# A decoder layer with an order written out by hand: another period string, idle products at both ends, and a first norm on two engines

## The chip, the core and the metric

The kernel runs on one core of a Trainium2 chip. A core has a matrix engine (TensorE, here PE, with its weight loads shown apart as PEld), a vector engine (VectorE, DVE), an activation engine (ScalarE, ACT), a general engine (GpSimd, POOL) and a queue processor that here only issues DMAs (SyncE, SP). Each engine works through its own instructions strictly in the order of the program, and waits for another engine by semaphores. The metric is the device time of one execution in microseconds (us); lower is better. Before the change the median of three runs is 2741.01 us (2739.99 to 2745.0).

## The reference

The input x is 128 sequences of 128 tokens with 256 features, all in float32. The layer does three things, each added to x: self-attention, cross-attention to a context of the same size, and a feed-forward part with 1024 hidden features. Each begins with a layer norm without weights.

```python
x = x + attn(layernorm(x), Wq, bq, Wk, bk, Wv, bv, Wo, bo)         # 16 heads of 16 features
x = x + xattn(layernorm(x), ctx, ctx, mask, wq, ..., wo_b)         # masked scores become 1e-9
x = x + ffn(layernorm(x), W_fc, ln_w, ln_b, W_proj)

# attention, per head: softmax(q k^T / 4) v, all heads side by side, then the output product
# ffn: weights are made ternary (-1, 0, 1) by their mean absolute value
h = gelu(x @ ternary(W_fc).T)
h = layernorm(h, ln_w, ln_b)
return h @ ternary(W_proj).T
```

## The kernel before

**Tiling.** Four sequences make a group; there are 32 groups. A group's x lies in SBUF as 128 tokens by 4 sequences by 256 features. Within a group, attention is done sequence by sequence (a "row"), for all 16 heads at once: the heads' score products use only 32 rows of the array each, so that four of them run side by side in four strips of the array (lines 680, 691, 752, 776); the product with the values (line 797) uses 32 columns each. All other products use the whole array.

**Streams.** The work is written as Python generators, "streams". Each `yield` ends a step, and each stream has one letter:

- `A`: attention, all rows of all groups in turn. A row's steps are `maxima` (scores, and their row maxima by DVE, line 702), `outputs` of the row before (line 797, copied out by ACT, line 800), `transposed_scores` (line 752) with `weights` (ACT's exponential, line 785), and `transposed_maxima` (line 719). Self rows of a group and cross rows of the group before it alternate by fours.
- `n`: `prepare_self`: load x, norm and transpose it (`transposed_copy`), then queries, keys and values. 17 steps a group.
- `k`: `prepare_keys`: load the context, then keys and values. 9 steps a group.
- `c`: `prepare_cross`: finish self-attention (`projected`: divide by the sums, output product, add to x), norm, and make the cross queries. 14 steps a group.
- `f`: `finish`: finish cross-attention, norm, then `hidden` (product and gelu) and `second` (norm of the hidden features, transposes, product), store. 36 steps a group. It runs for all groups but the last.
- `x`, `y`, `z`: the same for the last group, in three pieces of its rows (`finish_rows`).
- `w`, `t`: constants, and the ternary weights, once.

**Order.** Every engine's program is the order in which the steps are taken. This order is a string of letters: `START`, then `ORDER` once for each group of the middle, then `END` (line 851). `ORDER` has 112 letters, one group's worth of every stream: 36 A, 36 f, 17 n, 14 c, 9 k. Nothing else decides what comes before what. If an operand is late at a step, PE stands still, since the next step's products stand behind it in its queue.

**What joins the streams besides data.** All whole-array products and transposes take their output bank from one pool of three PSUM banks (`bank`, line 187). The fourth claim has to wait until the first bank is emptied by ACT or DVE. Scores have two tiles of their own, and the value product and the transposed maxima share one bank (`ps_av`). DVE empties the score tiles (line 702), copies values (line 365), adds products to x (lines 411, 503), makes the low halves of split operands (lines 425, 481), and computes the norms' statistics (lines 268, 269). POOL turns variances into reciprocal deviations (lines 274, 275) and applies the norms (line 279, four instructions for the four sequences of a group). SP issues all DMAs.

**The beginning.** The first group's x is loaded first. `transposed` takes its statistics in two steps, has POOL compute the deviations and apply the norm to the four sequences in the third, and then transposes the result on PE (line 297) in two steps.

Of the kernel before, what the change touches and what calls it, by code (L numbers as in the profile page):

```python
# [27 lines left out]
P = 128  # L28
# [21 lines left out]

START = (
    "nnnnnnwnwnnnwnnnAnAAnnAwnAAnAnAnAAAAAnnAAknnwAnnnnwnccnkAnnAAnnAnAkAcccckcAAcAnAAkccAccccntAAkAAnkAn"
    "AnAAnAkckAnnAnAcAnAnAnntAnAAAckccAccckkAAknAkAnknAnckcnAcAActAAftkAAAncAcAAntAAAffffAffnAnfnAnnAAnAn"
    "kAffnAAkfcfAffkfAAfknncffAAffffAkkfAnfcAcnfAfAffAAccfAc"
)
ORDER = (
    "ncfAfffAAkkAccAAcfcAnnfAAAccAffAAnnkAAnnAnfAnkAAAfffAfffnAAkcnnAnnAnAfkfkcAffffffAAfffAfffAfccccfffA"
    "fkfkAAAncfAn"  # L60
)
END = (
    "cfAfAffAfAcAcffcAfAAckAAxcAkcfffAAfffAAkfAAAAAkffkAcfAcAfffffAffAffccfffAcckcfckfAffAfAkkAfcAcfAAffc"
    "cAcfcAfAfkAAffAkAkfkAAAAfAfAffffAAxxAffAxAfffAxfffyfAfffffyfxAyffffAfxyxxxzxyfxfffzffyxzzffxxxxyyzxx"
    "yyzzzyzzz"
)


# [1 line left out]
def tile_decoder_layer(ctx: ExitStack, tc: tile.TileContext, a: dict, out: bass.AP):  # L70
    nc = tc.nc
    n_groups = a["x"].shape[0] // G
# [16 lines left out]
    def load_group(b):  # L89
        x = p_in.tile([P, G, D], F32, name="x", tag="x")  # L90
        nc.sync.dma_start(x, a["x"][b * G : (b + 1) * G].rearrange("g s d -> s g d"))
        held[b] = x
# [52 lines left out]
    ident = const.tile([P, P], F32, name="ident")  # L145
# [41 lines left out]
    def bank(name):  # L187
        return ps_mm.tile([P, 512], F32, name=name, tag="mm")
# [44 lines left out]

    def constants():

        attention_biases(w_self, "attn")
        yield
        output_bias(w_self)
        yield
        attention_biases(w_cross, "xattn")  # L240
        yield
        output_bias(w_cross)
        yield
        masks()
        yield

        row_of = const.tile([P, 4], F32, name="row_of")
        for n in range(4):  # L250
            rows = ident_strips[:, :, n:12:4]
            nc.vector.tensor_reduce(row_of[:, n : n + 1], rows, AX.XY, ALU.add)
            nc.vector.tensor_copy(add_max[:, n], row_of[:, n : n + 1].to_broadcast([P, P]))
        for i in range(2):
            rows = ident_strips[:, :, 4 * (i + 1) : 12]
            nc.vector.tensor_reduce(minus[:, i : i + 1], rows, AX.XY, ALU.add, negate=True)
        nc.gpsimd.memset(negms["cross"], 0.0)
        for v in values[1:]:
            clear_values(v)
        yield  # L260


    def statistics(src, rows, n, agg, at=0):
        for i, j in enumerate(rows):
            pieces = max(1, n // 512)
            stats = p_stat.tile([P, pieces, 6], F32, name="stats", tag="stats")
            for k in range(pieces):
                nc.vector.bn_stats(stats[:, k], src[:, j, k * n // pieces : (k + 1) * n // pieces])  # L268
            nc.vector.bn_aggr(agg[:, at + i], stats.rearrange("p i s -> p (i s)"))  # L269

    def deviation(agg, g):

        rstd = p_stat.tile([P, g], F32, name="rstd", tag="rstd", bufs=6)
        nc.gpsimd.tensor_scalar(rstd, agg[:, :, 1], LN_EPS, None, ALU.add)  # L274
        nc.gpsimd.tensor_tensor(rstd, rstd, minus_half.to_broadcast([P, g]), ALU.pow)
        return rstd

    def apply(engine, dst, src, agg, rstd, j):
        engine.tensor_scalar(  # L279
            dst[:, j], src[:, j], agg[:, j, 0:1], rstd[:, j : j + 1], ALU.subtract, ALU.mult  # L280
        )

    def transposed(x, evacuate):

        agg = p_stat.tile([P, G, 2], F32, name="agg", tag="agg", bufs=6)
        statistics(x, (0, 1), D, agg)
        yield
        statistics(x, (2, 3), D, agg, 2)
        rstd = deviation(agg, G)
        xn = p_act.tile([P, G, D], F32, name="xn", tag="xn", bufs=1)  # L290
        for j in range(G):
            apply(nc.gpsimd, xn, x, agg, rstd, j)
        yield
        for c in range(CC):
            pt = bank("pt")
            for j in range(G):
                nc.tensor.transpose(pt[:, j * P : (j + 1) * P], xn[:, j, c * P : (c + 1) * P], ident)  # L297
            evacuate(c, pt)
            if c == 0:
                yield  # L300

    def transposed_copy(x):
        xn_t = []

        def evacuate(c, pt):
            if c == 0:
                xn_t.append(p_act.tile([P, CC, T], F32, name="xn_t", tag="xn_t"))
            nc.scalar.copy(xn_t[0][:, c], pt)

        yield from transposed(x, evacuate)  # L310
        return xn_t[0]

    def product_halves(w, o, src_t, name):
# [55 lines left out]
    def queries(w, xn_t, unit):  # L369
        for o in range(CC):  # L370
            pq = yield from product_halves(w["q"], o, xn_t, "pq")
            if o == 0:
                qt = unit["q"] = p_act.tile([P, CC, T], F32, name="qt", tag="qt", bufs=3)
            nc.scalar.activation(qt[:, o], pq, AF.Identity, bias=w["bq"][:, o : o + 1], scale=Q_SCALE)
            if o == 0:
                yield
# [169 lines left out]
    def prepare_self(b):  # L546
        if b:
            load_group(b)
        yield
        x = held[b]  # L550
        xn_t = yield from transposed_copy(x)
        yield
        unit = ready["self", b] = {}
        yield from queries(w_self, xn_t, unit)
        yield
        yield from keys_values(w_self, xn_t, unit)
        add_row(x, w_self["bo"])
# [255 lines left out]
    def attention():  # L813
        w_t = added = None
        for i in range(-1, 2 * G * (n_groups + 1) + 1):
# [17 lines left out]
            if cross and here:  # L833
                w_t = weights(here[0], s, added_here)
                yield

    def all_groups(steps_of_group, groups=n_groups):
        for b in range(groups):
            yield from steps_of_group(b)
            yield  # L840
# [4 lines left out]
        "k": all_groups(prepare_keys),  # L845
        "c": all_groups(prepare_cross),
        "f": all_groups(finish, n_groups - 1),
        "w": constants(),
        "t": ternary_weights(),
    } | {letter: finish_rows(j0, n_rows) for letter, j0, n_rows in PIECES}  # L850
    for letter in START + ORDER * (n_groups - 4) + END:
        next(streams[letter])

    assert all(next(stream, None) is None for stream in streams.values())
# [42 lines left out]
```

## Time and profile before

| view | value |
|---|---|
| median of the runs | 2741.01 us |
| profiled execution, device time | 2739.6 us |
| its span, first to last instruction | 2737.6 us |
| PE busy | 2676.8 us (98%) |
| DVE busy | 2115.0 us (77%) |
| ACT busy | 1577.8 us (58%) |
| POOL busy | 1337.7 us (49%) |
| mean granted PE clock | 0.998 |

The profiled execution took 2739.6 us, 2.0 us more than its span and 1.4 us less than the median of the runs. A busy share is an average over the beginning, the 28 middle periods and the end. Matmuls are pipelined, and their ends are modelled: a PE that is shown as busy may still be held up for a few tenths of a microsecond. So PE's work is better read from one step's start to the next one's start.

The page cuts the span into 40 slices of 68 us: PE is busy nine tenths or more in all but the first (seven) and the last two (eight). DMAs keep the 16 DMA engines busy for a fifth of the time.

### The profile page before, as it was taken

The page shows a single profiled execution, that of the slowest core. Times are in us where ns is not written, and L with a number is a line of the kernel's source. Part 1 is how long each engine was busy: PE and PEld are TensorE (multiplying, and loading weights), DVE is VectorE, ACT ScalarE, POOL GpSimd, SP SyncE. Part 2 cuts the span into 40 slices and gives each one's busy share as a digit, 9 for nine tenths or more (in the row PEclk, how much of TensorE's full clock was granted, in tenths as well). Part 3 has the DMA queues.
Part 4 walks back from the last instruction along what each step waited for, and adds up shares of the span by engine and source line. Part 5 has one row for each costly group of instructions (what it writes and reads, how often), then busy time and mean ns, then how long its engine had stood idle before and what let it go on. Part 6 is the DMA issues. An engine that isn't in the chain of part 4 may idle for free.

```text
span 2737.6 us, 77047 instructions
## 1 busy us (share of the span) xinstructions
PE 2676.8 (98%) x32845; PEld 1917.6 (70%) x32845; DVE 2115.0 (77%) x3914; ACT 1577.8 (58%) x2508; POOL 1337.7 (49%) x1427
## 2 busy tenths in 40 slices
PE   7999999999999999999999999999999999999988
PEld 4567777777777777776777776777776777777666
DVE  4677787777887777887777887777877778877777
ACT  3455665655665556666556666556666556656546
POOL 2344554544554444554445545445545445545443
PEclk9999999999999999999999999999999999999999
DMA  4121111221121221122211212211112211212210
GB/s 110 41 50 35 46 44 49 57 56 31 46 48 50 57 49 35 41 53 53 57 42 41 42 49 57 57 42 41 42 49 58 57 32 47 47 49 50 50 26 16
DMA packets 110045, 130.28 MB, mean 48 GB/s; under 512 B 32264, under 2 KB 69000, under 8 KB 109704
## 3 DMA queue, kind: packets, MB, share of 16 engines
q1 hardware_dynamic: 109704, 125.37, 19.0%
q8 instruction: 259, 4.24, 0.6%
q14 instruction: 82, 0.67, 0.1%
HBM read 71.38 MB, written 18.84 MB: 33 GB/s over the span
## 4 chain that ended last, share of the span: by engine, by line
PE 89%; DVE 7%; issue 2%; POOL 1%; ACT 1%; DMA 0%; DVEq 0%; ACTq 0%; POOLq 0%; SPq 0%
PE st L752 10%; PE av L797 9%; PE pq L317 9%; PE s L691 9%; PE ph L436 9%; PE py L494 8%; PE pk L317 8%; PE po L329 8%; PE pv L329 8%; PE pt L297 3%; PE pg L470 2%; PE s L680 2%; PE st L776 2%; DVE mx L702 1%; DVE g L481 1%
## 5 line engine op out<-in xcount | busy, mean ns | idle before, releaser
L702 DVE TENSOR_REDUCE mx<-s 128x8 f32<-128x1024 f32 x512 | 601.0, 1215 | 82.2 <-PE s L691 81.8
L785 ACT ACTIVATE w_t<-st 128x1024 f32<-128x1024 f32 x512 | 496.7, 1022 | 200.7 <-PE st L776 121.4
L274 POOL TENSOR_SCALAR rstd<-agg 128x4 f32<-128x4 f32 (+2 forms) x163 | 38.8, 238 | 969.0 <-DVE agg L269 964.7
L279 POOL TENSOR_SCALAR xn<-x,agg,rstd 128x256 f32<-128x256 f32 x380 | 459.4, 1222 | 9.9
L762 DVE COPY_PREDICATED_SCALAR st<-masked_t,masked_score 128x1024 f32 x256 | 316.1, 1280 | 67.7 <-PE st L752 67.6
L407 POOL TENSOR_TENSOR o_raw<-o_raw,factors 128x256 f32<-128x256 f32 x252 | 181.3, 745 | 382.3 <-DMA factors<-by_head 277.7
L800 ACT COPY raw<-av 128x512 f32<-128x512 f32 x256 | 150.7, 589 | 314.7 <-PE av L797 306.9
L479 ACT ACTIVATE g<-pg,ln_w 128x256 fp32r<-128x256 f32 (+1 forms) x520 | 205.4, 472 | 175.6 <-PE pg L470 163.3
L691 PE MATMUL s<-kt,qt 32*128 32x256 f32 x4096 | 298.0, 401 | 3.2 <-ACT w_t L785 2.2
L494 PE MATMUL py<-w_proj,g 128*128 128x256 f32 x2048 | 279.6, 289 | 1.3 <-DVE g L481 0.8
L797 PE MATMUL av<-w_t,v 128*32 128x128 f32 x8192 | 277.8, 276 | 0.5 <-DVE q_max L724 0.5
L797 PEld LDWEIGHTS av<-w_t,v 128*32 128x32 f32 x8192 | 209.6, 110 | 97.3 <-issue 80.5
L436 PE MATMUL ph<-w_fc,xn 128*128 128x512 f32 x1024 | 259.6, 403 | 5.2 <-ACT g L443 2.6
L494 PEld LDWEIGHTS py<-w_proj,g 128*128 128x128 f32 x2048 | 254.0, 189 | 13.2 <-issue 1.3
L279 POOL TENSOR_SCALAR g<-g,agg,rstd 128x1024 f32<-128x1024 f32 x63 | 241.1, 3826 | 6.6
L481 DVE SCALAR_TENSOR_TENSOR g<-pg,ln_w,g 128x256 fp32r<-128x256 f32 (+1 forms) x520 | 212.5, 469 | 30.5 <-ACT g L479 30.3
L691 PEld LDWEIGHTS s<-kt,qt 32*128 32x128 f32 x4096 | 187.0, 184 | 63.2 <-issue 39.7
L436 PEld LDWEIGHTS ph<-w_fc,xn 128*128 128x128 f32 x1024 | 184.5, 188 | 59.9 <-DVE xn L425 10.3
L752 PEld LDWEIGHTS st<-q_max,kt 32*128 32x128 f32 x4096 | 129.2, 186 | 61.0 <-DVE negm_self L713 42.5
L268 DVE BATCH_NORM_STATS2 stats<-g 128x6 f32<-128x512 f32 x256 | 160.9, 670 | 0.8 <-ACT g L443 0.8
L443 ACT ACTIVATE g<-ph 128x512 f32<-128x512 f32 x256 | 146.5, 599 | 25.8 <-PE ph L436 24.5
L752 PEld LDWEIGHTS st<-qt,kt 32*128 32x128 f32 x4096 | 128.1, 186 | 46.3 <-DVE mx L702 26.4
(129 smaller groups left out, 4610.6 us busy)
## 6 DMA issues: line engine op xcount, KB each, us to landing
o_raw<-raw SPq DMA_DIRECT2D x504, 64.0 KB
factors<-by_head SPq DMA_DIRECT2D x126, 256.0 KB
x<-in_x_dram SPq DMA_DIRECT2D x32, 512.0 KB
ctx_t<-in_ctx_t_dram SPq DMA_DIRECT2D x32, 512.0 KB
out_dram<-x SPq DMA_DIRECT2D x31, 512.0 KB
sums<-raw SPq DMA_DIRECT2D x126, 16.0 KB
by_head<-r SPq DMA_DIRECT2D x63, 32.0 KB
raw_w<-in_w_fc_t_dram SPq DMA_DIRECT2D x1, 1024.0 KB
```

Of the source, the lines that this page charges most:

```text
L279: engine.tensor_scalar(dst[:, j], src[:, j], agg[:, j, 0:1], rstd[:, j : j + 1], ALU.subtract, ALU.mult)
L317: nc.tensor.matmul(out, w[:, c, o * P : (o + 1) * P], src_t[:, c], start=(c == 0), stop=(c == CC - 1))
L329: nc.tensor.matmul(rows[:, j], src_t[:, c, (j0 + j) * P : (j0 + j + 1) * P], w[:, c], start=(c == 0), stop=(c == CC - 1),)
L436: nc.tensor.matmul(ph, xn_parts[i][:, c, (j0 + j - at) * P : (j0 + j - at + 1) * P], w_fc[:, c, n * 512 : (n + 1) * 512], start=((i, c) == ...
L481: nc.vector.scalar_tensor_tensor(parts[1][:, f0 + f, tok], pieces[:, f], scales[f], parts[0][:, f0 + f, tok].bitcast(F32), ALU.mult, ALU.s ...
L494: nc.tensor.matmul(rows[:, j], parts[i][:, f, j * P : (j + 1) * P], w_proj[:, f], start=((i, f) == terms[0]), stop=((i, f) == terms[-1]),)
L691: nc.tensor.matmul(s[r // 2][:, r % 2, 2 * o : 2 * o + 2], qt[strip, o, tok], kt[strip, o, :, tok], start=(stage == "self"), stop=True, sk ...
L702: nc.vector.tensor_reduce(mx[:, 2 * half : 2 * half + 2], s[half], AX.X, ALU.max, negate=True)
L752: nc.tensor.matmul(s[r // 2][:, r % 2, n], kt[strip, n // 2, n % 2, tok], added[strip, n // 2, n % 2] if stage == "self" else qt[strip, n ...
L762: nc.vector.copy_predicated(s[half].rearrange("p r n q -> p (r n) q"), masked_t[:, None, :].to_broadcast([P, 8, P]), masked_score[:, :, No ...
L785: nc.scalar.activation(w_t[:, 2 * half : 2 * half + 2], s[half], AF.Exp)
L797: nc.tensor.matmul(av[32 * r : 32 * r + 32, n], v[:, j, head : head + 32], w_t[:, r, n], start=True, stop=True)
```

## The change

There are three parts.

1. **The strings.** `START`, `ORDER` and `END` are all replaced. The new `ORDER` again has 36 A, 36 f, 17 n, 14 c and 9 k, in another sequence, and the streams stand in other phases to each other when it begins: the new `START` takes 89 A, 70 n, 35 c, 23 k and 21 f (before: 89 A, 68 n, 35 c, 23 k, 29 f). `ORDER` is run 27 times rather than 28, and `END` has 335 letters rather than 209, since one more group is in it.
2. **Idle products.** A new stream `d` appears 30 times in `START` and 8 times in `END`, never in `ORDER`. A step of it takes a bank from the pool of three and does four transposes of the identity matrix into it. Nothing reads the result.
3. **The first group's norm.** For group 0 in `prepare_self` the norm is applied by DVE and POOL in turn (sequences 0 and 2 by DVE, 1 and 3 by POOL). All other groups keep POOL alone.

```diff
 START = (
-    "nnnnnnwnwnnnwnnnAnAAnnAwnAAnAnAnAAAAAnnAAknnwAnnnnwnccnkAnnAAnnAnAkAcccckcAAcAnAAkccAccccntAAkAAnkAn"
...
+    "ndddnddnnnwdnnnnnnnnwknwAnddAAdnndnAdndndAAddAAwnndAAndAAnAAAdwdnAnnnwnntncnAddnkcAAkndAtkknAAccccAc"
...
 ORDER = (
-    "ncfAfffAAkkAccAAcfcAnnfAAAccAffAAnnkAAnnAnfAnkAAAfffAfffnAAkcnnAnnAnAfkfkcAffffffAAfffAfffAfccccfffA"
-    "fkfkAAAncfAn"
+    "kcfAAkkAfAkffcAcfffAAcncfAAfffAAccAffAAfknAfnfAAnnAAnfnAcnAnnnAffAAfAfncAfnfkkAAccAcAcnAncffAAfnffff"
+    "fAffffnAkAkf"
 )
 END = (
...
-    "yyzzzyzzz"
+    "fAfcdAAAffdfAffAkkAffAfAccfffAccAcfAncffAAAAnAdAAfffnAffAfnfnkcnnckAAnffnAfffAffccfkAccfnAAfcnAffAfA"
...
+    "AcfcfckkcfkkfAfAffcfAkkcffccccfAAfAAffAfAAAAAAfffAfdffAAdxxdAffAxAdffxfAfffAffffffyydAfyxffffAfyxxxz"
+    "xfxxfyffzffyzzyxffzxxxxzzxyxyyzyzzz"
 )
...
-    def transposed(x, evacuate):
+    def transposed(x, evacuate, engines=(nc.gpsimd,)):
...
-            apply(nc.gpsimd, xn, x, agg, rstd, j)
+            apply(engines[j % len(engines)], xn, x, agg, rstd, j)
...
-        xn_t = yield from transposed_copy(x)
+        engines = () if b else ((nc.vector, nc.gpsimd),)
+        xn_t = yield from transposed_copy(x, *engines)
...
+    def idle_products():
+        for _ in range((START + END).count("d")):
+            rows = bank("idle")
+            for j in range(4):
+                nc.tensor.transpose(rows[:, j * P : (j + 1) * P], ident, ident)
+            yield
...
+        "d": idle_products(),
...
-    for letter in START + ORDER * (n_groups - 4) + END:
+    for letter in START + ORDER * (n_groups - 5) + END:
```

More of the change, by code (lines that the diff above doesn't have):

```diff
@@ L53 @@
 START = (
-    "nnnnnnwnwnnnwnnnAnAAnnAwnAAnAnAnAAAAAnnAAknnwAnnnnwnccnkAnnAAnnAnAkAcccckcAAcAnAAkccAccccntAAkAAnkAn"
-    "AnAAnAkckAnnAnAcAnAnAnntAnAAAckccAccckkAAknAkAnknAnckcnAcAActAAftkAAAncAcAAntAAAffffAffnAnfnAnnAAnAn"
-    "kAffnAAkfcfAffkfAAfknncffAAffffAkkfAnfcAcnfAfAffAAccfAc"
+    "ndddnddnnnwdnnnnnnnnwknwAnddAAdnndnAdndndAAddAAwnndAAndAAnAAAdwdnAnnnwnntncnAddnkcAAkndAtkknAAccccAc"
+    "cAnkkAAAkkdccAccncctAAkkAAtdnAnAnAAnnAAcnnAncAAnAAnkAdcAAAcccAknccAkAAknAnAnnkAnccndAAAkkAAccfAnAcnA"
+    "cnAAntAfAAffAfkfAfAnfdnAAdAnkAcdnkAAffnAnnAnAfffAcffkAAnAncfAkcAAcfcAfdAfAnnffc"
 )
 ORDER = (
-    "ncfAfffAAkkAccAAcfcAnnfAAAccAffAAnnkAAnnAnfAnkAAAfffAfffnAAkcnnAnnAnAfkfkcAffffffAAfffAfffAfccccfffA"
-    "fkfkAAAncfAn"
+    "kcfAAkkAfAkffcAcfffAAcncfAAfffAAccAffAAfknAfnfAAnnAAnfnAcnAnnnAffAAfAfncAfnfkkAAccAcAcnAncffAAfnffff"
+    "fAffffnAkAkf"
 )
 END = (
-    "cfAfAffAfAcAcffcAfAAckAAxcAkcfffAAfffAAkfAAAAAkffkAcfAcAfffffAffAffccfffAcckcfckfAffAfAkkAfcAcfAAffc"
-    "cAcfcAfAfkAAffAkAkfkAAAAfAfAffffAAxxAffAxAfffAxfffyfAfffffyfxAyffffAfxyxxxzxyfxfffzffyxzzffxxxxyyzxx"
-    "yyzzzyzzz"
+    "fAfcdAAAffdfAffAkkAffAfAccfffAccAcfAncffAAAAnAdAAfffnAffAfnfnkcnnckAAnffnAfffAffccfkAccfnAAfcnAffAfA"
+    "fffffkkAAfkfckAAnffAnnAAnffffAfAcxfcfAccAAcAAcfAAffAAfffAfAAkAAAAkfkcAkfcAffAAfkAfAffffffAffAAAkcfkc"
+    "AcfcfckkcfkkfAfAffcfAkkcffccccfAAfAAffAfAAAAAAfffAfdffAAdxxdAffAxAdffxfAfffAffffffyydAfyxffffAfyxxxz"
+    "xfxxfyffzffyzzyxffzxxxxzzxyxyyzyzzz"
 )
@@ L300, in transposed, with transposed_copy @@
                 yield
-    def transposed_copy(x):
+    def transposed_copy(x, *engines):
         xn_t = []
@@ L308, in evacuate @@
             nc.scalar.copy(xn_t[0][:, c], pt)
-        yield from transposed(x, evacuate)
+        yield from transposed(x, evacuate, *engines)
         return xn_t[0]
```

## The prediction

> **What bounds the kernel now.** I read first the sums over three stretches: the beginning (from PE's first instruction to the first letter of `ORDER`), the 28 middle periods, and the end. Columns: stretch, its length, then busy time of PE, PEld, DVE, ACT, POOL, the granted clock, DMA share, GB/s.
>
> ```profile
> 226.96:2544.28 2317.32, 2307.56 (x28677) 1658.72 (x28673) 1823.09 (x3364) 1377.10 (x2185) 1167.84 (x1232) 1.00 0.20 48
> 9.81:226.96 217.15, 199.74 (x2274) 129.90 (x2275) 148.77 (x269) 98.71 (x147) 87.99 (x95) 0.98 0.22 53
> 2544.28:2737.60 193.32, 169.48 (x1901) 128.95 (x1899) 139.67 (x263) 100.67 (x176) 77.22 (x86) 0.98 0.13 32
> ```
>
> PE is idle for 2317.3 - 2307.6 = 9.8 us in the whole middle, for 17.4 us in the beginning (and the 9.8 us before it), for 23.8 us in the end. The middle is PE's; the two ends are chains in which PE waits. Next, the chain of work that ended last and PE's list of waits over the middle:
>
> ```profile
> 367.02 3.89 PE ph L436 x16
> ...
> 2518.37 3.88 PE ph L436 x16
> ```
> ```profile
> PE pk L317 <- DVE g L481: 7.5, 26, 0.3
> ```
>
> The same place of the string comes back after (2518.37 - 367.02) / 26 = 82.74 us: the period. In it PE is seen waiting once, for 0.3 us: a product waits until DVE has emptied a bank. To see PE's own work, I took the timeline of one period and read each step from its start to the next one's start (start, us, instruction):
>
> ```profile
> 1268.45 1.17 PE L752 MATMUL st<-qt,kt 32*128 32x128 f32 x32
> 1269.55 1.12 PE L317 MATMUL pk<-xn_t,attn_wk 128*128 128x512 f32 x2
> 1270.51 1.03 PE L329 MATMUL pv<-attn_wv,xn_t 128*128 128x256 f32 x4
> 1271.38 0.27 PE L719 MATMUL pn<-ident,negm_cross 128*128 128x128 f32 x1
> 1271.48 1.03 PE L329 MATMUL pv<-attn_wv,xn_t 128*128 128x256 f32 x4
> 1272.44 0.58 PE L776 MATMUL st<-negm_t,add_max 32*128 32x128 bf16 x16
> ```
>
> Line 752 takes 1.10 us, 317 0.86 to 0.96, 329 0.86 (0.96 when a product in strips follows), 719 0.11. The other steps, read so: 797 1.01, 691 1.08 (1.44 with its mask products of line 680), 776 0.33, 494 1.99, 436 0.91, four transposes 0.44. One period has 16, 16, 8, 4, 8, 14 steps of lines 317, 329, 436, 494, 719 and transposes, and 8, 8, 4, 4, 4 of 752, 797, 691 plain, 691 masked, 776: together 78.1 us. Twenty changes from a whole-array step to one in strips cost 0.09 each (1.9), and the first whole-array step after strips about 0.1 where another follows (1.5). That is 81.5 us; in the old order line 494 follows 329 directly twice, some 0.14 us cheaper each time: 81.2. The period thus loses 82.7 - 81.2 = **1.5 us**.
>
> **The change, part by part.** *The period string.* The steps are the same 112, so PE's 78.1 us stay. I count again 20 changes into strips, and no 494 behind 329: 81.5 us. What remains are the late operands. For every step I set PE's time between producer and consumer against what the operand needs (ACT 0.6 to 1.0, DVE 0.5 to 2.4, POOL 4 x 1.22, DMAs by their own rows) with all that DVE, ACT, POOL and SP have queued ahead of it. Done for the old string, this gives shortfalls at three places: at letters 8 to 12 (0.5 us: DVE's two row maxima, 2.4 us, stand ahead of a bank and of the transposes' norm), at 57 (0.2), and from 101 to 110 (0.9: bank emptied late by DVE, where the trace shows the 0.3 us wait). The sum, 1.6, answers to the 1.5 lost. For the new string it gives **one**: letters 12 to 21, `fcAcfff`. Transposes, two transposes of `c` and row maxima are followed by a fourth claim of a bank after 0.44 + 1.08 + 0.09 + 0.44 = 2.05 us of PE work. The bank is emptied by DVE's two instructions of 0.47 us, behind the statistics, maxima, value copies, `q_max` and norm that have piled up since letter 1; they are 0.9 us late, and the scores and query product behind it not more so. One more step is just in time; everything else has 0.2 us or more to spare, SP's moved DMAs (sums and raw outputs at letter 4, stores at 43, factors at 45 and 56) and POOL's norms among it. So 81.5 + 0.9 to 1.0 = **82.5 us**, 0.24 less than now; times 27 = **-6.5 us**. The count is good to about 0.4 us a period, so +4 to -17.
>
> *First group's norm.* POOL does four pieces now:
>
> ```profile
> 8.51 4.85 POOL L279 TENSOR_SCALAR xn<-x,agg,rstd 128x256 f32<-128x256 f32 x4
> ```
> ```profile
> L279 POOL TENSOR_SCALAR xn<-x,agg,rstd 128x256 f32<-128x256 f32 x380 | 459.4, 1222 | 9.9
> ```
>
> PE's first real product waits for the last of them. The trace has DVE do such a piece at line 648 (four times, 0.41 us each). With two pieces each, POOL ends after 2 x 1.22 = 2.44 us and DVE beside it before that: 4.85 - 2.44 = **-2.4**. DVE waits for POOL's deviation with the constants' small instructions behind it; the score maxima need DVE only at 26 us. The Trainium skill speaks against it: SBUF — State Buffer (Who interferes with whom) has VectorE and GpSimd share a port pair, which a `tensor_scalar` on VectorE in a two-port mode holds for its whole length, so that the other engine stands still. Then the four add up: 2 x 1.22 + 2 x 0.41 = 3.27, and the gain is 1.6. But the timelines of the middle show both engines at line 279 at once:
>
> ```profile
> 1374.15 3.79 POOL L279 TENSOR_SCALAR g<-g,agg,rstd 128x1024 f32<-128x1024 f32 x1
> ```
> ```profile
> 1374.62 1.27 DVE L279 TENSOR_SCALAR g<-g,agg,rstd 128x1024 f32<-128x1024 f32 x1
> ```
>
> POOL's instruction takes its usual 3.79 us (3.79 is also the median of all 63) with DVE's wholly inside it; it is DVE that stretches, from 0.80 in other places to 1.27. At that rate DVE's two pieces still end within POOL's 2.44 us. I take 2.4.
>
> *Idle products.* Four transposes are 0.44 us of PE, 38 steps 16.6 us. In the beginning, 30 of them (13.1 us) stand among steps that leave PE idle for 17.4 us now (37 us when steps are read start to start). Five of the end's eight stand between the last attention rows, in idle time too. Three stand in its first fifty letters, where PE has nothing to spare: 1.3 us. A few more will meet PE with work ready: I take **+2 us**, from 0 to 16.6 if no cover is left. Each claims a bank and can wait for its emptying, with all of PE queued behind; the next real product would claim that bank otherwise. What they can bring is PE's clock:
>
> ```profile
> 14.57 3.65 PE L317 MATMUL pq<-xn_t,attn_wq 128*128 128x512 f32 x4
> ...
> 18.91 1.88 PE L317 MATMUL pq<-xn_t,attn_wq 128*128 128x512 f32 x4
> ```
> ```profile
> 96.45:99.86 3.41, 3.41 (x20) 2.17 (x20) 2.16 (x4) 0.00 (x0) 0.00 (x0) 0.50 0.02 5
> 2605.25:2608.66 3.41, 3.41 (x24) 2.20 (x23) 2.47 (x6) 2.59 (x3) 2.44 (x3) 0.50 0.00 0
> ```
>
> The same product takes twice as long at 14.57, and four stretches of 3.41 us run at clock 0.50 (82.8, 96.45, 2605.25, 2731.54), each behind one in which PE had waited. Half of five stretches is 8.3 us, the most that a clock kept up could give; no `d` stands near the last. TensorE: Matmul & The Clock Gate (Part 4: PE-mode transpose) says that transposes do not count as PE activity for the gate: by that rule the gain is nothing. The trace's eight transposes before 14.57 left the clock low, but filled only 2.5 us of 4.7, so it does not decide. I take one stretch, **-1.5**.
>
> *The ends otherwise.* Eight steps of `f` go from the beginning to the end, and a whole period with them; that moves PE work without adding any. The letters after the last A are 41 as before, nine of them f: the tail stays as it is. Dead time (steps read start to start) is 37 + 38 us; another order can give or take some 10 us of it, and I take **0**.
>
> Sum: -6.5 - 2.4 + 2 - 1.5 = **-8.4 us** on a span of 2737.6: 2729.2, or 2731.2 as device time of the profiled execution (2739.6). The runs' median lies 1.4 us above that: 2741.0 - 8.4 = **2732.6 us**.
>
> **The rivals.**
>
> *Fuller ends.* With f lagging eight steps more, the end has more whole-array work to put between the last attention rows, where PE idles now. If a fifth of the 75 us of dead time goes, 15 us: 2732.6 - 15 = 2718. For it: the end's idle 23.8 us. Against it: the unchanged last 41 letters, in which some 10 us of that idle time lie.
>
> *Idle products in the way.* If half of the 38 meet PE with work ready (8.4 us) and the clock does not care for transposes, the sum is -6.5 - 2.4 + 8.4 = -0.5: 2740.5, no change. For it: the beginning reaches nine tenths busy within its first 68 us slice or two.
>
> *A longer period (slower).* DVE is busy 77%; where row maxima and predicated copies meet with bank emptying, one instruction more in the queue makes a chain of late banks that my count of covers sees as just in time (seven places of the new string have 0.2 to 0.3 us to spare). Each 0.1 us a period costs 2.7 us. At 82.8 us the period's gain is gone; from 83.06 us on it outweighs the rest, and the kernel is over 0.2% slower. At 83.2: 27 x 0.46 = 12.4 - 1.9 = +10.5, 2751 us.
>
> *The change doesn't do what it says* only in one point: the clock, told above.
>
> **How the numbers follow.** Chances: as summed 0.50 (its own range 2724 to 2735), fuller ends 0.15, products in the way 0.15, longer period 0.20. A change of 0.2% (5.5 us) is about what a measurement of this kernel can tell from none: faster is below 2735.5, slower above 2746.5. So faster 0.65, same 0.15, slower 0.20. The range leaves out the better part of the fuller ends and of the longer period: 2717 to 2751.
>
> **What would show it.** The period, from one `ph` of line 436 in the chain to the same one a period later: 82.5 us, with PE's wait on `g` of line 481 now before the transposes of line 470. The first transposes end near 11.9 us rather than 14.3. The idle transposes appear as line 470's kin on `ident`; whether half-clock stretches at 83, 96 and 2605 are gone tells if they count. I am wrong if the period is above 82.74, if the beginning plus end, less one period, has grown by more than 2 us, or if new waits of PE on `mx` (line 702) or on factors appear in the middle.

## The result, and the profile after

The changed kernel takes 2761.54 us in the median (2760.59 to 2762.67) where the kernel before takes 2741.99 us on the same chip: a ratio of 1.0072, 95% interval 1.006 to 1.0083. It is slower by 0.6 to 0.8%. Predicted was 2732.6 us, and the time lies above the range (2717 to 2751). The profiled execution's span grew from 2737.6 to 2759.2 us, by 21.6 us.

The changed file is longer, so line numbers have moved by 2 to 4: 317 is now 319, 443 is 445, 445 is 447, 470 is 472, 481 is 483, 691 is 695, 702 is 706, 752 is 756, 776 is 780, 785 is 789. Experiments built on the changed kernel can be shifted by one or two more.

The sums over the three stretches come first, as before the change (stretch, its length, busy time of PE, PEld, DVE, ACT, POOL, granted clock, DMA share, GB/s):

```profile
9.80:215.29 205.49, 199.54 (x2341) 134.25 (x2342) 144.66 (x264) 95.30 (x138) 79.05 (x91) 1.00 0.23 55
215.29:2468.54 2253.25, 2240.64 (x27650) 1620.65 (x27648) 1770.90 (x3246) 1382.65 (x2161) 1128.55 (x1188) 1.00 0.20 47
2468.54:2760.00 291.46, 263.37 (x2987) 198.05 (x2987) 208.91 (x388) 157.18 (x266) 125.24 (x133) 0.97 0.13 33
```

The middle now holds 27 periods, one fewer than before; that group's work stands in the end. A middle period is 2253.25 / 27 = 83.45 us long, against 2317.32 / 28 = 82.76 before: 27 x 0.69 = 18.7 us of the 21.6. The rest is in the beginning and the end: 215.29 + 290.66 (to the span's end at 2759.2) = 505.95 us, against 226.96 + 193.32 and one old period of 82.76, 503.04. That is +2.9. So nearly the whole loss is the period, and the chain of work that ended last says the same, with the same place of the string at both ends, (2456.83 - 287.06) / 26 = 83.45:

```profile
287.06 3.89 PE ph L438 x16
...
2456.83 3.89 PE ph L438 x16
```

PE's waits over the middle (who waits, for what; us in total, times, longest):

```profile
PE pq L319 <- DVE g L483: 11.9, 25, 0.8
```

Once in nearly every period, and up to 0.8 us long, a query product waits for its bank, which DVE empties in line 483. The prediction's first sign, a wait of PE ahead of the transposes of line 472, is not in this list.

Read as in the prediction, each step from its start to the next one's start less PE's own work, the middle loses this much in each period (means without the first period, whose seam still follows `START` and not `ORDER`):

```text
letters of ORDER (from 0)            before   after
3        scores, then value product     -     0.56
14-17    scores, then transposes        -     0.25
20       transposed scores, then pq     -     0.74
92       scores, then value product     -     0.22
other places, in sum                  1.50    0.12
sum                                   1.50    1.89
```

PE's own work is 83.45 - 1.89 = 81.56 us, as predicted (81.5). What is lost is 1.9, not 0.9 to 1.0, and a third of it lies at a letter at which the prediction had everything on time.

Who is late at letter 3? The groups of ACT instructions of before (line, operation, count | busy us, mean ns | idle before) hold two kinds of function-table load in the middle, and those of after four:

```profile
L431 ACT ACT_TABLE_LOAD x65 | 83.4, 1283 | 1.1
L445 ACT ACT_TABLE_LOAD x65 | 83.4, 1283 | 1.1
```
```profile
L433 ACT ACT_TABLE_LOAD x65 | 83.4, 1283 | 0.8
L447 ACT ACT_TABLE_LOAD x65 | 83.4, 1283 | 1.2
L789 ACT ACT_TABLE_LOAD x28 | 35.9, 1283 | 17.0 <-issue 16.9
L445 ACT ACT_TABLE_LOAD x28 | 35.9, 1283 | 0.5
```

Lines 433 and 447 are the preloads that the program writes ahead of and behind the four gelus of two hidden rows. The other 56 loads are in no line of the program: they were put in front of an exponential (789) and of a gelu (445), since the new `ORDER` ends with `fAffffnAkAkf`, and an `A` that needs an exponential stands between the third and the fourth gelu. The timeline of ACT at the seam of two periods (start, length, instruction; idle before it):

```profile
1462.74 1.58 ACT L445 ACTIVATE g<-ph 128x512 f32<-128x512 f32 x3
1464.95 1.28 ACT L789 ACT_TABLE_LOAD   x1 [0.63 <-issue]
1466.24 1.94 ACT L789 ACTIVATE w_t<-st 128x1024 f32<-128x1024 f32 x2
1468.07 1.45 ACT L353 ACTIVATE kt<-pk,xattn_bkh,parity 128x512 f32<-128x512 f32 x2
1469.54 1.28 ACT L445 ACT_TABLE_LOAD   x1
```

and of PE in the same place:

```profile
1464.47 0.40 PE L780 MATMUL st<-negm_t,add_max 32*128 32x128 bf16 x16
...
1467.65 1.71 PE L695 MATMUL s<-kt,qt 32*128 32x256 f32 x16
```

ACT is done with the third gelu at 1464.32 and stands idle for 0.63 us. The load starts only when the exponential's operand is complete (line 780 ends at 1464.87), and the exponentials start 1.4 us after their operand. They free the tiles that the next scores (line 695) fill, and these take 1.71 us here where they take 1.15 with their tiles free.

### The profile page after: what moved, and what is told of

Read it like the earlier page. It is cut to its first block, busy times and chain, and to the rows that moved or that the text cites. A ratio compares the mean times of both kernels' runs of the same rounds, so it can differ in the third digit from the quotient of the medians.

```text
span 2759.2 us, 77407 instructions
## 1 busy us (share of the span) xinstructions
PE 2708.5 (98%) x32997; PEld 1957.3 (71%) x32997; DVE 2128.7 (77%) x3916; ACT 1636.4 (59%) x2564; POOL 1337.5 (48%) x1425
## 3 DMA queue, kind: packets, MB, share of 16 engines
q1 hardware_dynamic: 109704, 125.37, 18.7%
## 4 chain that ended last, share of the span: by engine, by line
PE 82%; DVE 14%; ACT 1%; issue 1%; POOL 1%; DMA 0%; SPq 0%; DVEq 0%; POOLq 0%; ACTq 0%
PE py L496 9%; PE s L695 9%; PE pq L319 9%; PE po L331 9%; PE ph L438 9%; PE pk L319 8%; PE st L756 8%; PE av L801 7%; PE pv L331 6%; DVE mx L706 5%; PE pt L299 2%; PE pg L472 2%; DVE g L483 2%; PE s L684 2%; PE st L780 2%; DVE stats L270 2%
## 5 line engine op out<-in xcount | busy, mean ns | idle before, releaser
L695 PE MATMUL s<-kt,qt 32*128 32x256 f32 x4096 | 322.4, 403 | 1.4 <-ACT w_t L789 1.4
L438 PE MATMUL ph<-w_fc,xn 128*128 128x512 f32 x1024 | 271.9, 412 | 1.0 <-ACT g L445 0.7
L695 PEld LDWEIGHTS s<-kt,qt 32*128 32x128 f32 x4096 | 204.0, 184 | 74.3 <-issue 46.0
L728 DVE SCALAR_TENSOR_TENSOR q_max<-pn,max_rows,qt 128x256 f32<-128x256 f32 x256 | 111.0, 475 | 108.8 <-PE pn L723 108.7
L756 PE MATMUL st<-q_max,kt 32*128 32x128 f32 x4096 | 157.4, 283 | 1.0 <-DVE mx L706 0.9
L270 DVE BATCH_NORM_STATS2 stats<-x 128x6 f32<-128x256 f32 x384 | 155.6, 405 | 2.7 <-DMA x<-in_x_dram 2.6
```

What stands on the lines that cost most here:

```text
L438: nc.tensor.matmul(ph, xn_parts[i][:, c, (j0 + j - at) * P : (j0 + j - at + 1) * P], w_fc[:, c, n * 512 : (n + 1) * 512], start=((i, c) == ...
L695: nc.tensor.matmul(s[r // 2][:, r % 2, 2 * o : 2 * o + 2], qt[strip, o, tok], kt[strip, o, :, tok], start=(stage == "self"), stop=True, sk ...
L756: nc.tensor.matmul(s[r // 2][:, r % 2, n], kt[strip, n // 2, n % 2, tok], added[strip, n // 2, n % 2] if stage == "self" else qt[strip, n ...
```

## The experiments

Theory: the table load that stands between the last maxima product and its exponential makes the scores late, and everything else that is lost at the seam follows from that. Rivals: DVE's queue is too long there whatever ACT does (the prediction's own rival, a longer period); the idle products or the new first norm cost the time; the number of table loads costs it, wherever they stand.

**Without the idle products.** In the changed kernel:

```diff
+START, END = START.replace("d", ""), END.replace("d", "")
```

> The changed kernel without its 38 idle products. Theory 1 (the loss sits in the 27 middle periods, each 83.46 us rather than 82.74): the period stays at 83.46 us; the beginning's products stood in dead time and the end's eight cost up to 4 us, so the time stays within 2757 to 2763 us. Rival (the idle products stand in PE's way): 38 x 0.44 us = 16.6 us come back, 2745 us. A third view (they keep PE's clock up in the beginning): stretches at half clock return there and the time rises by 2 to 4 us.

Measured: 2757.79 us (2755.87 to 2760.06), ratio to before 1.0064 (1.0049 to 1.0079). The middle begins 2.7 us earlier (212.6 instead of 215.3), the end is 0.9 us longer, and the period is unchanged: it still loses 0.56 at letter 3 and 0.80 at letter 20. The idle products aren't the cause of the longer period. By the medians they cost 3.75 us in all.

**The first norm by POOL alone.** In the changed kernel:

```diff
-        engines = () if b else ((nc.vector, nc.gpsimd),)
+        engines = ()
```

> The changed kernel with the first group's norm on POOL alone, as before the change. If the 2.4 us that POOL saves at the start carry through to the end: +2.4 us, 2764 us. If a later wait of the beginning swallows them (score maxima, the second group's norm): no change, 2761 to 2762 us.

Measured: 2764.05 us (2761.55 to 2764.45), ratio 1.0084 (1.0069 to 1.01): 2.5 us above the changed kernel by the medians, with overlapping intervals; the middle begins at 216.84, 1.55 us later. The period is the same. The other way round, the two-engine norm alone in the kernel before:

> The kernel before with only the two-engine norm of the first group. Prediction's step: first transposes 2.4 us earlier and the whole 2.4 us shorter, 2738.5 us, ratio 0.9991. By two instructions that exclude each other: 1.6 us. Rival (the start's gain is lost again before the period begins, because a later operand decides): 2741 us, ratio 1.000.

Measured: 2736.98 us (2733.43 to 2740.76), ratio 0.9989 (0.9983 to 0.9996), so 1.1 to 4.7 us faster than before. The norm is a gain, as predicted.

**No gelu behind the exponential.** In the changed kernel the fourth gelu of the second pair of rows is left out; an exponential of the scaled input stands in its place, with other values and the same place in ACT's queue, and the Exp preload stands behind the third:

```diff
-                nc.scalar.activation(g[:, j, n * 512 : (n + 1) * 512], ph, AF.Gelu)
-                if j + n == n_rows:
+                last = n_rows == 2 and j0 == 2 and j + n == 2
+                nc.scalar.activation(g[:, j, n * 512 : (n + 1) * 512], ph, AF.Exp if last else AF.Gelu, scale=0.01 if last else 1.0)
+                early = n_rows == 2 and j0 == 2
+                if (j, n) == (1, 0) if early else j + n == n_rows:
                     nc.scalar.preload_act_table(AF.Exp)
```

> The changed kernel with ACT's last gelu of the second hidden half computed as an exponential of the scaled input instead (its values are wrong), and the table for exponentials loaded one step earlier: the order of all steps stays, and the two function table loads that the exponential of an attention row and the gelu after it cost in each period (line 789 and line 445, 28 each in the trace) are gone. Theory 1a (these loads make the exponential late, which holds the next scores, 0.56 us a period): the period falls from 83.46 to about 82.9 us, the time to 2746 us. Rival (DVE's queue at letters 12 to 21 is what binds, and the loads hide behind it): the period falls by less than 0.2 us, the time stays above 2757 us.

Measured: 2725.19 us (2723.87 to 2725.72), ratio 0.9944 (0.9929 to 0.9959). The period falls to (2429.78 - 213.65) / 27 = 82.08 us and loses 0.49 in place of 1.89: nothing at letter 3, 0.05 at letter 20. So the losses at 3 and at 20 have one root on ACT, and the old count of what DVE has queued is no obstacle. This run takes away two loads and moves one; the next three tell the number from the place.

**The exponential behind all four gelus.** In the changed kernel, an `f` is moved within the end of `ORDER`:

```diff
-    "fAffffnAkAkf"
+    "fAfffffnAkAk"
```

> The changed kernel with the last hidden product of a group moved from the end of the period (letter 111) up to its three sisters (letter 106), so that no attention exponential falls between gelus. The function table loads are gone as in the run with an exponential for a gelu, but 0.9 us of PE work no longer lies between the attention row's mask product and the next scores. If the loads alone made the scores late: the period falls by 0.5 us, 2748 us. If the exponential's own 2.04 us are what the scores wait for: the cover lost eats the loads saved, and the period stays within 0.2 us of 83.46 us, the time within 2756 to 2767 us.

Measured: 2765.43 us (2764.39 to 2767.79), ratio 1.0093 (1.0076 to 1.011). All loads without a line of their own are gone but two of 56, and it is no faster than the changed kernel: 2.04 us are lost in a period, 0.77 at letter 3 and 0.67 at letter 20. ACT's timeline shows why:

```profile
1467.28 0.60 ACT L445 ACTIVATE g<-ph 128x512 f32<-128x512 f32 x1 [0.31 <-PE ph L438]
1467.90 1.28 ACT L447 ACT_TABLE_LOAD   x1
1469.19 1.94 ACT L789 ACTIVATE w_t<-st 128x1024 f32<-128x1024 f32 x2
```

The preload is queued behind the fourth gelu, and that gelu waits for PE. The mask product (line 780) starts at 1468.15 and takes 0.40 us, so the exponential now starts 0.64 us after its operand, not 1.4. But the moved product's 0.91 us of PE work no longer stands between the operand and the next scores, and for them the exponential is no earlier than it was. So this run changes two things, and it shows only that in this place the missing loads don't make up for the missing work of PE.

**The Exp preload one gelu earlier.** In the changed kernel, a third preload in the second pair of rows; nothing else moves:

```diff
-                if j + n == n_rows:
+                if j + n == n_rows or (n_rows, j0, j, n) == (2, 2, 1, 0):
                     nc.scalar.preload_act_table(AF.Exp)
```

> The changed kernel with one more load of the exponential's function table, put right behind the third gelu of the second hidden half, so that it is there before the attention row's exponential; the fourth gelu still loads its own table again. As many table loads as in the changed kernel, one of them earlier by 0.6 us, none left out, and nothing computed differently. If what costs is that the exponential comes late for the next scores: the scores are on time, DVE's queue behind them too, and the period falls from 83.46 to 82.2 us, the time to 2727 us. If what costs is the number of loads (ACT's time) or the late fourth gelu: the period stays within 0.3 us, the time above 2753 us.

Measured: 2733.06 us (2730.79 to 2733.94), ratio 0.997 (0.9959 to 0.998): faster than both kernels. The period is (2433.83 - 215.17) / 27 = 82.17 us, as expected, with 0.49 lost; that the time is 6 us above the 2727 us expected lies in the end of the kernel, told below. The early load is all that differs from the changed kernel, so the late exponential is the cause. The groups of ACT's loads:

```profile
L447 ACT ACT_TABLE_LOAD x96 | 123.2, 1283 | 1.7
L433 ACT ACT_TABLE_LOAD x65 | 83.4, 1283 | 0.8
L445 ACT ACT_TABLE_LOAD x32 | 41.1, 1283 | 0.5
```

That is 193 loads in these groups where the changed kernel has 186, and 28 us less time. ACT's and PE's timelines at the same place of the string:

```profile
1527.23 1.58 ACT L445 ACTIVATE g<-ph 128x512 f32<-128x512 f32 x3
1528.83 1.28 ACT L447 ACT_TABLE_LOAD   x1
1530.12 1.94 ACT L789 ACTIVATE w_t<-st 128x1024 f32<-128x1024 f32 x2
```
```profile
1528.95 0.40 PE L780 MATMUL st<-negm_t,add_max 32*128 32x128 bf16 x16
...
1532.13 1.15 PE L695 MATMUL s<-kt,qt 32*128 32x256 f32 x16
```

The load now follows the third gelu at once, in the 0.63 us in which ACT stood idle, and 0.52 of its 1.28 us are over when the exponential's operand comes (line 780 ends at 1529.35). The exponential starts 0.77 us after its operand instead of 1.4, and that is enough: the scores take 1.15 us again. A load that is written as a preload doesn't wait for the operand of the exponential behind it; the one that is put in front of the exponential did. The rule of the Trainium skill, ScalarE: Activation LUTs (Table sets: the hidden batching unit), to do all calls of one set together, would have chosen the joined string over this one; here the joined string is 32 us slower, though it also has less of PE's work ahead of the scores. Its price for a switch, 2.66 us with a drain (What ACT_TABLE_LOAD costs), isn't seen either: a load takes 1.28 us; in the changed kernel's timeline the next ACTIVATE starts 0.01 us after it (1466.24), and the load at 1469.54 starts 0.02 us after the ACTIVATE ahead of it ends.

**Copies on ACT.** The cross values are copied by ACT in the changed kernel, to take 0.68 us twice off DVE at the seam:

```diff
-            nc.vector.tensor_copy(heads[:, :, :, 0:HD], rows.rearrange("p j (h d) -> p j h d", d=HD))
+            copy = nc.scalar.copy if w is w_cross else nc.vector.tensor_copy
+            copy(heads[:, :, :, 0:HD], rows.rearrange("p j (h d) -> p j h d", d=HD))
```

> The changed kernel with the copies of the cross values out of their banks (line 367) on ACT instead of DVE, two of which stand in DVE's queue at letters 5 and 10, just ahead of the late bank; ACT gets 2.4 us more a period. If DVE's queue is the second half of the loss (0.7 to 0.8 us at letters 14 to 21): that part goes, the scores stay 0.56 us late, and the period is 82.7 us, 2741 us. If ACT, where the scores' delay comes from, is short too: the copies come late there, and the period stays at 83.3 us or above, 2757 us or more.

Measured: 2761.91 us (2761.81 to 2762.39), ratio 1.008 (1.0065 to 1.0095), no gain: 0.58 lost at letter 3, 0.5 at 14 to 16, 0.54 at 20. DVE has the norm of the hidden features done earlier, and then waits for ACT, whose high halves of line 482 come behind the copies:

```profile
1474.88 0.81 DVE L281 TENSOR_SCALAR g<-g,agg,rstd 128x1024 f32<-128x1024 f32 x1
1477.24 0.88 DVE L484 SCALAR_TENSOR_TENSOR g<-pg,ln_w,g 128x256 fp32r<-128x256 f32 x2 [1.55 <-ACT g L482]
```

Work moved from DVE to ACT at this place only changes which of them is late.

**Two loads in the kernel before.** An Exp and a Gelu preload between the third and fourth gelu of the second pair of rows, where the old string has no exponential:

```diff
                 if j + n == n_rows:
                     nc.scalar.preload_act_table(AF.Exp)
+                elif n_rows == 2 and (j0, j, n) == (2, 1, 0):
+                    nc.scalar.preload_act_table(AF.Exp)
+                    nc.scalar.preload_act_table(AF.Gelu)
```

> The kernel before with the two table loads of the changed kernel added on ACT, exponential and then gelu, between the third and the fourth gelu of the second hidden half: 2.57 us of ACT a period, in an order that has no exponential there. If table loads cost by their own length anywhere: +1 us or more a period, 2770 us. If they cost only where an exponential or a bank waits behind them with no cover: here the next scores stand 6 us of PE work behind the exponential, and the period rises by less than 0.2 us, below 2747 us.

Measured: 2796.41 us (2796.07 to 2800.18), ratio 1.0208 (1.0193 to 1.0224). A period loses 3.42 us instead of 1.50, at letters 97 to 100 and 106. I had taken the loads to be covered there, and they are not. The largest of PE's waits over the middle, once a period, is for a bank that DVE empties late, when it adds a product to x:

```profile
PE pg L473 <- DVE x L411: 14.4, 26, 0.6
```

So two loads more cost 1.9 us a period in this place. With the early preload the changed kernel also has six loads a period, two more than the run without the reload, and both lose 0.49. So the number of loads doesn't decide; their place in the order does.

**Another string in the kernel before.** I wrote a third string with a count of durations and queues like the prediction's, to see whether such a count can find a good one:

```diff
-    "ncfAfffAAkkAccAAcfcAnnfAAAccAffAAnnkAAnnAnfAnkAAAfffAfffnAAkcnnAnnAnAfkfkcAffffffAAfffAfffAfccccfffA"
-    "fkfkAAAncfAn"
+    "kcfAfnffAAkfcAAcccAAnAccnAAfAfAAnfkAAnkAnAnkAnAAnfffAffffnAnncAAnkAnAfnfkAffcffAffAfffffffAcccAfcfnA"
+    "AfffAnfkkAAc"
```

> The kernel before with START and END as they are and another ORDER, found by moving letters so that by the steps' durations in the trace of the kernel before, function table loads among them, no operand is late. No idle products, norm on POOL. If a period is PE's own 81.2 to 81.5 us once nothing is late: 28 x 1.3 = 36 us less than before, 2700 to 2712 us. If durations taken from one order do not hold in another (DVE and POOL stretch each other's instructions where they meet): new late operands, a period of 82 to 83 us, 2715 to 2745 us.

Measured: 2985.89 us (2977.0 to 2995.12), ratio 1.0897. It loses 10.4 us a period, mainly at letters 6, 70 and 102. The largest of PE's waits over the middle:

```profile
PE pg L470 <- DVE g L481: 117.5, 48, 2.5
```

In one instance, at 1512 us, DVE waits 0.38 us for scores and then works 2.35 us at their row maxima; the emptying of the bank that PE needs is queued behind them, and PE waits 2.53 us. Both expectations missed by far, though this count had the table loads among its durations. Which step of it failed was not followed further; the run shows that such a count, the prediction's own method, can be wrong by 10 us a period.

**The best of both.** The early preload, without the idle products of the beginning:

```diff
+START = START.replace("d", "")
```

> The changed kernel with the Exp preload ahead of the third gelu of the second hidden half (as in a_early_exp), and without the idle products of the beginning; those of the end stay. Theory (the late exponential costs the period, the idle products of the beginning cost PE time of their own): the period stays at 82.2 us and the beginning becomes some 2.7 us shorter, as between the changed kernel and a_no_idle, so 2733 - 2.7 = 2730 us, ratio about 0.996. Rival (idle products only fill time that is idle anyway): 2733 us, ratio 0.997.

Measured: 2728.43 us (2726.8 to 2732.54), ratio 0.9964 (0.9951 to 0.9978). The middle begins at 211.4 instead of 215.2. Its end, though, is 296.5 us long, as in the run with the early preload alone (297.3), where the changed kernel's is 290.7. In the end no exponential stands between these gelus, and the early preload only makes the fourth gelu wait for two loads. ACT and PE there, in the run with the early preload alone:

```profile
2512.08 1.28 ACT L447 ACT_TABLE_LOAD   x1
...
2514.35 1.28 ACT L445 ACT_TABLE_LOAD   x1
2515.64 0.60 ACT L445 ACTIVATE g<-ph 128x512 f32<-128x512 f32 x1
```
```profile
2516.29 1.99 PE L319 MATMUL pk<-ctx_t,xattn_wk 128*128 128x512 f32 x4 [2.47 <-ACT g L445]
```

PE waits 2.47 us for a bank that this gelu empties. So the early preload was confined to the 28 groups that have the exponential, still without the idle products of the beginning:

```diff
-                if j + n == n_rows or (n_rows, j0, j, n) == (2, 2, 1, 0):
+                if j + n == n_rows or (early and j + n == 1 and j == 1):
...
-            gs.append((yield from hidden(xn_parts, j0)))
+            gs.append((yield from hidden(xn_parts, j0, early=j0 == 2 and b < n_groups - 4)))
```

> a_best with the early Exp preload only for the 28 groups in which an exponential follows the third gelu of the second hidden half; the last groups, in which none follows, keep the changed kernel's single preload there. Theory (a preload costs where it stands between two gelus with no exponential to serve: in a_early_exp the end is 297.3 us long against 290.7 in the changed kernel, 2.6 and 2.8 us of it before the transposes of the hidden features and in the attention row behind them): the period stays at 82.2 us, the end goes back by 6 us, 2722 us, ratio 0.994. Rival (the end is longer for another reason, such as the clock): 2728 us as a_best, ratio 0.996.

Measured: 2724.22 us (2723.24 to 2725.82), ratio to before 0.9936 (0.9923 to 0.995). The end is 291.4 us long, the period 82.13. It is the fastest of these kernels; the run without the reload, which leaves a gelu out, is level with it. With the exponential's table loaded in time, and the beginning's idle products left out, the change is a gain of 0.5 to 0.8%.

## Why the prediction was wrong

**The step that failed is the period's "late operands".** The prediction took what an operand needs from ACT as "ACT 0.6 to 1.0". For an exponential between two gelus it is 1.28 more, and no table load stands anywhere in its working, though the trace of before had 131 of them. The old string has no exponential between the gelus of a pair of rows, the new one has, once a period; that could be read from the strings. Whether a count with this term would have come out right is not shown: the third string was laid with such a count, and missed by far. The sign came out wrong: 27 x 0.69 = +18.7 us where the prediction has -6.5. With the load out of the way the same string gives 27 x (82.17 - 82.76) = -15.9 us.

**How 0.56 us late becomes 1.4 us lost (1.89 less 0.49).** Each link can be read by setting the changed kernel beside the run with the early preload, at a place of the string that DVE reaches 64.51 us later there (the same statistics start at 1464.09 and at 1528.60). DVE at the seam, after:

```profile
1474.61 0.69 DVE L367 COPY v<-pv 128x512 f32<-128x512 f32 x1
1475.22 1.50 DVE L281 TENSOR_SCALAR g<-g,agg,rstd 128x1024 f32<-128x1024 f32 x1
...
1477.43 2.34 DVE L706 TENSOR_REDUCE mx<-s 128x8 f32<-128x1024 f32 x2
1479.80 1.07 DVE L717 COPY negm_self<-mx 128x8 f32<-128x8 f32 x2
```

and with the early preload:

```profile
1538.91 0.68 DVE L367 COPY v<-pv 128x512 f32<-128x512 f32 x1
1539.51 0.80 DVE L281 TENSOR_SCALAR g<-g,agg,rstd 128x1024 f32<-128x1024 f32 x1
...
1541.01 2.35 DVE L706 TENSOR_REDUCE mx<-s 128x8 f32<-128x1024 f32 x2
1543.39 0.45 DVE L717 COPY negm_self<-mx 128x8 f32<-128x8 f32 x2
```

PE is 0.6 us late, so the value products come late, and DVE's value copy starts 0.2 us late (1474.61 against 1538.91 - 64.51 = 1474.40). With that DVE's norm starts 0.23 us behind POOL's, not with it:

```profile
1474.99 3.79 POOL L281 TENSOR_SCALAR g<-g,agg,rstd 128x1024 f32<-128x1024 f32 x1
1478.74 2.79 POOL L419 TENSOR_TENSOR x<-x,xattn_bo 128x256 f32<-128x256 f32 x4
```

DVE's instruction then takes 1.50 us instead of 0.80. So it goes throughout: of the changed kernel's 58 such pairs between 200 and 2600 us, DVE is 0.2 us behind in 26, which take 1.50 to 1.54 us, and 1.0 us or more behind in 28, which take 0.80 or 0.81. The maxima behind it are 0.93 us late, the copies of line 717 now meet POOL's line 419 (0.39 and 0.77 us, 1.07 in all, where the run with the early preload has 0.45), and the emptying of banks behind these is 1.7 us late. That is the wait of `pq` on line 483 at letter 20.

This place is one of the worse ones. The next period of the changed kernel, 83.81 us later, has the same norm of 1.50 us, but its second copy takes 0.16 us:

```profile
1563.61 0.47 DVE L717 COPY negm_self<-mx 128x8 f32<-128x8 f32 x2
```

In 11 of the 27 periods the second copy takes 0.76 or 0.77 us, and the step at letter 20 then takes 2.20 or 2.21 us. In 14 it takes 0.16, and the step takes 1.59 or 1.60. (The other two, with 0.45 and 0.16, have 1.28 and 1.43.) So the stretch of this one copy, 0.61 us, goes whole into the loss, and makes 0.25 of the 0.74 us a period.

That the late exponential is the root is shown, by the run without the reload and by the three with an early preload. That the copy of line 717 is a link is shown by these periods. That the rest of the loss at letter 20 goes through the stretched norm is only argued: the run that kept DVE's norm at 0.81 us in nearly all periods (copies on ACT) had made ACT late in its place.

The prediction's own shortfall, letters 12 to 21 with 0.9 to 1.0 us, isn't confirmed either. The changed kernel loses 0.25 + 0.74 = 0.99 us there, just the size predicted, but this is luck: without the late exponential 0.13 is lost at letter 14 and 0.05 at 20. The run with the early preload comes to 2733.06 us, the prediction was 2732.6, and this is an accident: its period is 0.33 us shorter than predicted (82.17, 8.9 us over 27 periods), and its beginning and end together are 512.4 us, 9.4 us longer than 503.0 where they should have been 1.9 us shorter.

**First norm.** -2.4 predicted, 1.1 to 4.7 us measured alone. The timelines of the beginning, after (POOL, then DVE):

```profile
8.51 2.58 POOL L281 TENSOR_SCALAR xn<-x,agg,rstd 128x256 f32<-128x256 f32 x2
```
```profile
8.43 0.90 DVE L281 TENSOR_SCALAR xn<-x,agg,rstd 128x256 f32<-128x256 f32 x2 [1.49 <-POOL rstd L277]
```

POOL's 4.85 us became 2.58. DVE's two pieces run beside it, 0.90 us from the first's start to the second's end: the first, begun before POOL, takes 0.41 us, the second 0.57. The reading from the row was the right one here; by two instructions that exclude each other it would have been 3.3 us. PE's first query product, at 14.57 us in the kernel before, starts at 12.18 with this norm alone and at 13.42 in the changed kernel: the 2.4 us are there, and the idle products put ahead of that product take half of them back.

**Idle products.** +2 predicted for PE's time and -1.5 for the clock. Measured is about +2 to +4 for both together, more than the +0.5 predicted: 3.75 us between the medians with and without them; in the two profiles +2.7 in the beginning and -0.9 in the end. The half-clock stretches of 83 and 96 us are gone in the changed kernel, as the prediction hoped, but the idle products didn't do it. From 80 to 100 us the granted clock is 0.83 before, 1.00 after, and 1.00 in the run without them. A new stretch of 6.83 us at clock 0.50 stands in the end of both, at 2666 us, at attention rows in which PE waits.

**The ends otherwise.** 0 predicted. In all the ends grew by 2.9 us where -1.9 had been predicted for norm, idle products and clock. The sign that the prediction named for itself, more than 2 us, has come true as well, though it is a seventh of the loss.

**The rivals.** "A longer period" is the one that happened, and its price of 2.7 us for each 0.1 us a period was right: 18.7 us for 0.69. Its first threshold was not: by its own terms a period outweighs the other 1.9 us from 82.81 us on, and costs 5.5 us more than before from 83.01 on, not 83.06. It named DVE's queue as the cause. The cause is on ACT, and DVE's queue makes it larger. One more sum of the prediction is off, without bearing on the outcome: half of five stretches of 3.41 us is 8.5 us, not 8.3.

## What to carry to other kernels

When an order of work is changed, list for every engine what has to be switched between two neighbours in its queue, not only how long each takes: here one new neighbourhood, an exponential between two gelus, was worth 28 us (2761.5 against 2733.1) and turned a gain of 0.3% into a loss of 0.7%. What counted here was not the number of table loads but whether a load stood in time in which the engine was idle anyway. Here that was a preload right behind the last use of the old table, and only where an exponential follows. A position that is late by half a microsecond can cost more than twice that (1.4 us for 0.56 here), when it moves an instruction of VectorE onto one of GpSimd.

## What the runs showed of the hardware

**The clock and transposes.** The prediction weighed the statement of TensorE: Matmul & The Clock Gate (Part 4: PE-mode transpose) that transposes don't count for the clock gate, and could not decide it. These transposes of a float32 identity can count. Six runs begin with 20 of them back to back. In three, the changed kernel among them, all but the first stay at 213 or 214 ns from one start to the next, and the granted clock is first up at 17 us. In the other three the rate doubles on the way. One of these is the run with POOL's norm; its clock by stretches:

```profile
4.21:7.62 3.41, 0.92 (x8) 0.68 (x6) 2.59 (x12) 0.00 (x0) 0.51 (x2) 1.00 0.98 263
7.62:11.04 3.42, 0.50 (x2) 0.22 (x2) 0.25 (x2) 0.00 (x0) 3.31 (x4) 0.50 1.05 324
```

From one start to the next the gap is 268 ns once, then 213 or 214 twelve times, then 130, and the last five are 109 or 110: the rate doubles after some 3 us of idle products. In this run PE then has nothing to do until 9.8 us, and the next stretch is at half clock again. So they can raise the clock, not in every run, and in this kernel they raise it where no work follows.

**DVE and POOL at once.** The prediction argued from one row that DVE stretches to 1.27 us beside POOL. It is not one price. Begun 0.23 us after POOL, DVE's 0.80 us become 1.50; begun 0.47 after, 1.27; begun 1.0 after, 0.80. In these three cases it ends 1.73 to 1.81 us after POOL's start. Begun together or before, DVE keeps its 0.80 and POOL takes 4.32 instead of 3.79 us, as with the early preload:

```profile
1539.49 4.32 POOL L281 TENSOR_SCALAR g<-g,agg,rstd 128x1024 f32<-128x1024 f32 x1
```

SBUF — State Buffer (Who interferes with whom) says that beside a VectorE instruction in a two-port mode whichever of the two issues first holds the shared ports for its whole length, and the other stands still. For DVE begun 0.23 us behind POOL's 3.79 us that would be 3.56 us; measured is a stretch of 0.7. That these instructions run in such a mode is not shown here.
